# Edge groups of the destination attention: loaded in the graph convolution, coded and split in the first expert layer, transposed in the first attention

## The chip, the cores and the metric

The kernel is one program on one core of a Trainium2 chip. The metric is the time of one execution on the device in microseconds (us), of which the median over several runs is taken; lower is better. A core has five engines that run side by side, each through its own list of instructions in order: PE (TensorE, matrix products), DVE (VectorE), ACT (ScalarE), POOL (GpSimd) and SP (SyncE, which here only issues DMAs). DMAs are issued by SP and ACT on a queue of each, and by POOL where rows are gathered or scattered by index. A `Tile` layer places the instructions: the order in which the Python code traces them is a wish, and an instruction can be placed ahead of others once its data and its space in memory are there.

## What is computed

A network of four layers on a graph of 3125 nodes with 256 features and 100000 edges (`src`, `dst`, sorted by `dst`). Each layer has a graph part and an expert part:

```python
edge_index = jnp.stack([src, dst])
x = x + L0_gnn(layernorm(x), edge_index, edge_weight, ...)     # graph convolution + 2-layer MLP
x = x + L0_ffn(layernorm(x))                                   # 8 experts, 2 per token, 256 wide
x = x + L1_gnn(layernorm(x), edge_index, edge_attr_2, ...)     # attention over sources, 4 heads
x = x + L1_ffn(layernorm(x))                                   # 8 experts, 2 per token, 1024 wide
x = x + L2_gnn(layernorm(x), ..., edge_attr_3, edge_index)     # attention over destinations, 8 heads
x = x + L2_ffn(layernorm(x))                                   # 8 experts, 2 per token
x = x + L3_gnn(layernorm(x), ...)                              # 3 hops
x = x + L3_ffn(layernorm(x))                                   # 8 experts, 1 per token, with a capacity
```

The change concerns what the third graph part (`L2_gnn`) needs of the edges. For each edge it needs the source, the destination, the three attributes of `edge_attr_3`, and, since it takes a maximum over all edges of one destination, the knowledge of which neighbouring edges have the same destination.

## The kernel before

`x` stays in SBUF as 25 tiles of 128 nodes. Constants: `P` = 128, `CH` = 4, `G` = `CH`*`P` = 512 edges in a group, `NU` = 220 groups of edges sorted by destination (a group has edges of one destination tile only), `NCK` = `NU`*`CH` = 880.

The order of the work, with the times at which the profiled execution has it:

1. **Ranks and scatter** (0 to 1340 us). The edges' ranks by source and destination tile are counted, then POOL scatters the 100000 edges with 800 indirect DMAs (L955 in `scatter`) into the DRAM table `chunks`.
2. **Beside the scatter.** `groups_of_dst` works out where each group begins (`es_d`), how many edges it has left (`gd_left`) and the number of the group plus one (`gd_iu1`). `first_layer` makes the first products, `table_of_edges` writes the table of edges `sorted_d`. `load_groups` then loads the 220 groups with 220 DMAs of SP (16 KB each, 128 bytes a partition) into `raw_d` (178 to 379 us). `degrees` sums edge weights by source. Then come the two pieces of the change: `codes_of_groups` makes the gather index `idx_d` (L580), a mask of the real edges (L584), the code (L589 to L591: destination plus group number for real edges, minus the group number for the rest), its store to DRAM (`codes`, L599), and the destination within its tile `lo_d` (L601 to L607). `edge_rows` makes `er_lo` (L617) and splits the three attributes into three BF16 parts each (`split`, L260 to L265), and stores both to DRAM as `er_all` (L626, L627).
3. **Block building** (`blocks`, 518 to 1405 us): the edges are read back from `chunks` in pieces (`ch`) as the scatter gets on, turned into one-hot matrices (`bk_oh`, L1132; `bk_ow`, L1153) and products (L1162, L1165, summed at L1171), and stored as dense 128x128 blocks, `mats`.
4. **Graph convolution** (`gcn`, 1412 to 1745 us): for each of 25 destination tiles a load of 1.6 MB of blocks (`m`, three buffers, on SP), 25 matmuls (L1288), addition and scaling on DVE, a transpose (L1298) and its copy (`h7T`, L1299). In this loop `rows_of_edges` transposes 3 of 69 pieces of `er_all` a tile (PE transpose, copy on DVE and ACT in turn, store on the queue of ACT), after one load of all of `er_all` on the queue of ACT. After tile 2 `penalties` reads `codes` back (`pn_co`), compares neighbours (`pn_pen`, L639, L642) and stores the penalties in 16 DMAs. Then the two dense products follow, hidden layer `hT` of pool `l0g`, product L1317.
5. **First expert part** (`routed`, `moe`, 1735 to 1958 us): the router and the slots of tokens (`slots`, DVE), the store of normalised rows `xrows` (L1650, SP), then 28 groups of tokens in `experts`: weights on SP (L1545 to L1551, three buffers), gathers of rows on POOL (`xb`, L316, three buffers), transposes (L1565), products (L1575, L1582), scatter of results on POOL (L1589). `between(u)` is called after group u and adds the normalised rows to x (L1663).
6. **First attention** (`attention`, 1965 to 3400 us): a front (load of `ch`, L1710, and its transposes, projection weights, results of the experts read back, L1679, layer norm and projection), then `messages`: 276 steps with a load (`lb`, L1776, SP), a one-hot compare (`ot`, L1778, DVE), a gather by matmul (PE), a product (`m`, L1793, DVE), an addition (L1797, POOL), a copy (`ex`, L1798, ACT) and a store (`stash`, L1799, SP). Then come the sums.
7. The second expert part, the third graph part (3515 to 4625 us; it reads `idx_d`, `lo_d`, `lo_rows`, `att_rows`, `pens`), its experts, the hops and the last experts.

The `Tile` pools are stacks: a pool opened where another has been closed uses the same space, and its first writer waits for the last readers there.

Of the kernel before, what the change touches and what calls it, by code (L numbers as in the profile page):

```python
# [10 lines left out]
F32 = mybir.dt.float32  # L11
BF16 = mybir.dt.bfloat16
# [76 lines left out]
class Net:  # L89
# [231 lines left out]
    def sort_edges(self):  # L321
# [3 lines left out]
        with tc.tile_pool(name="sg", bufs=1) as keep:  # L325
# [17 lines left out]
            with tc.tile_pool(name="sr", bufs=1) as early:  # L343
                with tc.tile_pool(name="st", bufs=1) as gpool, \
                        tc.tile_pool(name="st_ps", bufs=1, space=PSUM) as psum, \
                        tc.tile_pool(name="l0x", bufs=2) as xp, tc.tile_pool(name="l0xps", bufs=2, space=PSUM) as xpsum:
                    starts = self.groups_of_dst(early, gpool, psum, wrong)
                    self.first_layer(xp, xpsum)
                    self.table_of_edges(0)
                    self.load_groups(early, starts)  # L350
                with tc.tile_pool(name="dg", bufs=1) as pool, \
                        tc.tile_pool(name="dg_ps", bufs=1, space=PSUM) as psum:
                    self.expert_buffers(pool)
                    self.degrees(pool, psum)
                    self.codes_of_groups(pool)
                    self.edge_rows(pool)
# [142 lines left out]
    def groups_of_dst(self, early, pool, psum, wrong):  # L499
# [54 lines left out]
        left = early.tile([P, NU], F32, name="gd_left")  # L554
        nc.vector.tensor_tensor(left, end, es, op=OP.subtract)
        iu1 = early.tile([P, NU], F32, name="gd_iu1")
        nc.vector.tensor_scalar(iu1, iu, 1.0, None, op0=OP.add)
        self.left, self.iu1 = left, iu1
        return es_i

    def load_groups(self, early, es_i):
# [3 lines left out]
        raw = early.tile([P, NCK, 8], F32, name="raw_d")  # L565
        rawg = raw.rearrange("p (u c) w -> p u c w", c=CH)
        last = []
        for u in range(NU):
            r = self.load_reg(SP, u, last[u - 8] if u >= 8 else None, es_i, 2 * E + G)
            last.append(nc.sync.dma_start(  # L570
                out=rawg[:, u], in_=self.tables[ds(r, G), :].rearrange("(p c) w -> p c w", c=CH)))
        self.raw_g = raw

    def codes_of_groups(self, pool):


        nc, const, raw, end, iu1 = self.nc, self.const, self.raw_g, self.left, self.iu1
# [2131 lines left out]
```

## Time and profile before

| | |
|---|---|
| median of 10 runs | 6101.39 us (6095.77 to 6106.09) |
| the profiled execution | 6100.68 us |
| its span | 6098.8 us |
| busy: PE, DVE, POOL, ACT | 4931.5, 3682.7, 2435.0, 2394.7 us |
| scatters L955 | 800, 984.1 us busy |
| groups' loads, 178 to 379 us | 220 on SP |
| graph convolution | 1412 to 1745 us |
| first experts on PE | 1818 to 1958 us |
| messages of the first attention | 2031 to 2370 us |

The profile comes from one execution. Its span is the time from the first to the last instruction on the engines; the execution's own time is 1.9 us longer. The profile says when each instruction ran and, where an engine was idle, which event ended the idle time (its releaser). "L955" is line 955 of the kernel; "chunks<-tb_pay,tb_row" are the names of what is written and read; "SPq" is the issuing of DMAs by SP. A group line gives a count, the busy time in us with the mean of one in ns, and then the idle time just before, with its releaser. A wait line gives us in total, how many times, and the longest. The granted clock is the share of full speed that PE was given.

### The profile page before, as it was taken

The page shows a single profiled execution, that of the slowest core. Times are in us where ns is not written, and L with a number is a line of the kernel's source. Part 1 is how long each engine was busy: PE and PEld are TensorE (multiplying, and loading weights), DVE is VectorE, ACT ScalarE, POOL GpSimd, SP SyncE. Part 2 cuts the span into 40 slices and gives each one's busy share as a digit, 9 for nine tenths or more (in the row PEclk, how much of TensorE's full clock was granted, in tenths as well). Part 3 has the DMA queues.
Part 4 walks back from the last instruction along what each step waited for, and adds up shares of the span by engine and source line. Part 5 has one row for each costly group of instructions (what it writes and reads, how often), then busy time and mean ns, then how long its engine had stood idle before and what let it go on. Part 6 is the DMA issues. An engine that isn't in the chain of part 4 may idle for free. (4 is left out here: it accounts for less than half of the span.)

```text
span 6098.8 us, 89424 instructions
## 1 busy us (share of the span) xinstructions
PE 4931.5 (81%) x24912; PEld 3978.8 (65%) x24912; DVE 3682.7 (60%) x7420; ACT 2394.7 (39%) x6080; POOL 2435.0 (40%) x2332
## 2 busy tenths in 40 slices
PE   5446777568977787999699789898985999699986
PEld 4334776566855786777588545555554887488775
DVE  6788998672142898999511458888887000432343
ACT  3454777561022212444322366666662222210121
POOL 3778777760006464000022177777770222000021
PEclk8657777668989898999699879999996999799988
DMA  3473234456527574222355476667663653798653
GB/s 83 106 17 35 61 95 112 116 141 174 155 82 214 168 219 153 76 75 75 110 184 180 153 230 196 198 197 202 198 195 98 203 181 128 209 241 238 172 191 121
DMA packets 987725, 912.52 MB, mean 150 GB/s; under 512 B 188483, under 2 KB 897573, under 8 KB 986422
## 3 DMA queue, kind: packets, MB, share of 16 engines
q1 hardware_dynamic: 873858, 716.08, 41.0%
q0 software_dynamic: 84736, 166.99, 11.2%
q10 hardware_dynamic: 28580, 23.10, 1.2%
q8 instruction: 223, 3.65, 0.3%
q14 instruction: 328, 2.69, 0.2%
HBM read 707.87 MB, written 288.94 MB: 163 GB/s over the span
## 5 line engine op out<-in xcount | busy, mean ns | idle before, releaser
L955 POOL DMA_INDIRECT chunks<-tb_pay,tb_row x800 | 984.1, 1230 | 337.1 <-issue 241.4
L316 POOL DMA_INDIRECT xb<-xrows,sl_tok x172 | 168.3, 978 | 1387.7 <-DVE sl_to L1522 1221.4
L316 POOL DMA_INDIRECT g<-table,idx_d x652 | 631.3, 968 | 215.7 <-issue 157.2
L1584 DVE TENSOR_TENSOR yb<-ps_o,eb 128x256 f32<-128x256 f32 x200 | 84.5, 423 | 953.0 <-PE ps_o L1582 934.1
L1575 PE MATMUL ps_h<-xe,ew 128*128 128x256 f32 x2528 | 584.4, 389 | 31.6 <-ACT xe L172 17.4
L1582 PE MATMUL ps_o<-ew,hT 128*128 128x256 f32 x2528 | 562.5, 379 | 0.0
L1171 DVE SCALAR_TENSOR_TENSOR bk_acc<-bk_acc,bk_on,bk_m 128x256 f32<-128x256 f32 x1102 | 527.5, 479 | 51.8 <-DVE bk_acc L1171 0.4
L1575 PEld LDWEIGHTS ps_h<-xe,ew 128*128 128x128 f32 x2528 | 481.4, 193 | 116.7 <-ACT xe L172 32.0
L1855 PE MATMUL ps_a<-rhs,oh 128*128 128x261 f32 x2208 | 510.1, 387 | 31.9 <-ACT rhs L1852 24.9
L2485 PE MATMUL ps_a<-h,m 128*128 128x512 f32 x1875 | 485.1, 408 | 56.9 <-DVE ln_st L202 45.7
L1165 PE MATMUL bk_m<-bk_ow,bk_oh 128*128 128x128 f32 x2208 | 512.5, 372 | 13.8 <-ACT bk_ow L1153 13.8
L1582 PEld LDWEIGHTS ps_o<-ew,hT 128*128 128x128 f32 x2528 | 477.1, 190 | 69.1 <-ACT hT L1577 4.2
L1577 ACT ACTIVATE hT<-ps_h,eb 128x256 f32<-128x256 f32 x632 | 297.2, 474 | 572.9 <-PE ps_h L1575 566.5
L1162 PE MATMUL bk_m<-bk_oh 128*128 128x128 f32 x1104 | 305.6, 369 | 242.3 <-DVE bk_acc L1171 222.1
L1855 PEld LDWEIGHTS ps_a<-rhs,oh 128*128 128x128 f32 x2208 | 409.9, 190 | 131.9 <-ACT oh_abs L1840 38.9
L2288 PE MATMUL ps_a<-wt,oh 128*128 128x264 f32 x1664 | 453.1, 419 | 48.2 <-ACT l_iota L2248 25.2
L1153 ACT ACTIVATE bk_ow<-bk_oh,ch 128x128 f32<-128x128 f32 x1104 | 363.9, 389 | 274.3 <-DVE bk_oh L1132 259.9
L2485 PEld LDWEIGHTS ps_a<-h,m 128*128 128x128 f32 x1875 | 350.9, 190 | 134.9 <-ACT h L2430 54.1
L1165 PEld LDWEIGHTS bk_m<-bk_ow,bk_oh 128*128 128x128 f32 x2208 | 425.4, 269 | 14.4 <-ACT bk_ow L1153 14.1
L1162 PEld LDWEIGHTS bk_m<-bk_oh 128*128 128x128 f32 x1104 | 236.6, 265 | 298.4 <-issue 177.1
L2288 PEld LDWEIGHTS ps_a<-wt,oh 128*128 128x128 f32 x1664 | 329.8, 204 | 145.5 <-DVE wt L2278 44.6
L2094 DVE SCALAR_TENSOR_TENSOR tt<-er,col,ps_hd 128x512 f32<-128x512 f32 x416 | 293.2, 743 | 178.2 <-PE ps_hd L2093 163.7
(611 smaller groups left out, 8996.5 us busy)
## 6 DMA issues: line engine op xcount, KB each, us to landing
m<-mats SPq DMA_DIRECT2D x99, 1600.0 KB
mats<-bk_acc SPq DMA_DIRECT2D x1103, 128.0 KB
ew<-in_L_ffn_W_dram SPq DMA_DIRECT2D x116, 1024.0 KB
hd<-rows SPq DMA_DIRECT2D x208, 256.0 KB
stash<-m SPq DMA_DIRECT2D x276, 136.0 KB
ms<-stash SPq DMA_DIRECT2D x276, 136.0 KB
lb<-src_rows SPq DMA_DIRECT2D x276, 128.0 KB
ew<-in_L_ffn_w_dram SPq DMA_DIRECT2D x28, 1024.0 KB
```

Source lines behind the costliest of these rows:

```text
L316: return self.nc.gpsimd.indirect_dma_start(out=out, out_offset=None, in_=table, in_offset=bass.IndirectOffsetOnAxis(ap=idx, axis=0))
L955: sc = nc.gpsimd.indirect_dma_start(out=self.chunks, out_offset=bass.IndirectOffsetOnAxis(ap=self.row[:, k : k + 1], axis=0), in_=self.pay ...
L1153: nc.scalar.mul(ow[:, i], of[:, k % 4 + i, 0, :], ch[:, c + i, 2:3])
L1162: nc.tensor.matmul(ps[:, i, 0, :], oh[:, c0 + i, 0, :], oh[:, c0 + i, 1, :], start=True, stop=True)
L1165: nc.tensor.matmul(ps[:, i, 1, :], of[:, c0 + i, 1, :], ow[:, i], start=True, stop=True)
L1171: nc.vector.scalar_tensor_tensor(new, acc[0], goes_on[:, k + i : k + i + 1], ps[:, i], op0=OP.mult, op1=OP.add)
L1575: nc.tensor.matmul(ps, w1[:, k, f * P : (f + 1) * P], xe[:, k, :], start=k == 0, stop=k == 1)
L1577: nc.scalar.activation(hT[:, f, :], ps, act, bias=b1[:, f : f + 1])
L1582: nc.tensor.matmul(ps, hT[:, f, j * P : (j + 1) * P], w2[:, f, :], start=f == 0, stop=f == FP - 1)
L1855: nc.tensor.matmul(ps, oh[:, c, :], rhs[:, c, :], start=c == 0, stop=c == CH - 1)
L2288: nc.tensor.matmul(po, oh[:, c, :], wt[:, c, :], start=c == 0, stop=c == CH - 1)
L2485: nc.tensor.matmul(pa.rearrange("p i d -> p (i d)"), m[:, j, :], h[:, j].rearrange("p i d -> p (i d)"), start=j == 0, stop=j == NT - 1)
```

## The change

- `groups_of_dst` writes `gd_left` and `gd_iu1` as one tile to DRAM (`left_d`) and keeps the starts of the groups.
- `load_groups` becomes a generator with one load at a time. It is moved into the loop of `gcn`, nine loads a tile, into a pool `sr` (28 KB a partition) that is opened at the start of `gcn` and kept until the first experts are done.
- `codes_of_groups` is called after group 1 of the first experts, `edge_rows` after group 3, both in a pool `cg` (some 41 KB a partition). `left_d` is read back for it.
- `rows_of_edges` is moved from `gcn` to the messages of the first attention, one piece every third step; it loads each piece of `er_all` by itself on SP, copies on ACT and stores on SP.
- `penalties` is moved from `gcn` to just before the messages. The message buffers in PSUM (`l1gps`) go from 4 to 3, and two small ones for the transposes are added.

```diff
@@ -340,20 +340,16 @@
                     self.rows_of_table(pool, self.tables[E + G :], rows)
                 self.ranks(keep, rows)
             self.load_x()
-            with tc.tile_pool(name="sr", bufs=1) as early:
-                with tc.tile_pool(name="st", bufs=1) as gpool, \
-                        tc.tile_pool(name="st_ps", bufs=1, space=PSUM) as psum, \
-                        tc.tile_pool(name="l0x", bufs=2) as xp, tc.tile_pool(name="l0xps", bufs=2, space=PSUM) as xpsum:
-                    starts = self.groups_of_dst(early, gpool, psum, wrong)
-                    self.first_layer(xp, xpsum)
-                    self.table_of_edges(0)
-                    self.load_groups(early, starts)
-                with tc.tile_pool(name="dg", bufs=1) as pool, \
-                        tc.tile_pool(name="dg_ps", bufs=1, space=PSUM) as psum:
-                    self.expert_buffers(pool)
-                    self.degrees(pool, psum)
-                    self.codes_of_groups(pool)
-                    self.edge_rows(pool)
+            with tc.tile_pool(name="st", bufs=1) as gpool, \
+                    tc.tile_pool(name="st_ps", bufs=1, space=PSUM) as psum, \
+                    tc.tile_pool(name="l0x", bufs=2) as xp, tc.tile_pool(name="l0xps", bufs=2, space=PSUM) as xpsum:
+                self.groups_of_dst(gpool, psum, wrong)
+                self.first_layer(xp, xpsum)
+                self.table_of_edges(0)
+            with tc.tile_pool(name="dg", bufs=1) as pool, \
+                    tc.tile_pool(name="dg_ps", bufs=1, space=PSUM) as psum:
+                self.expert_buffers(pool)
+                self.degrees(pool, psum)
             self.gcn_inputs()
             self.blocks()
 
@@ -496,7 +492,7 @@
                     tc.add_to_no_dep_group(f"radix{i}", sc.ins)
         nc.sync.dma_start(out=table[:E], in_=tabs[3])
 
-    def groups_of_dst(self, early, pool, psum, wrong):
+    def groups_of_dst(self, pool, psum, wrong):
 
 
         nc, const = self.nc, self.const
@@ -551,30 +547,33 @@
         nc.vector.tensor_scalar(other, wrong[0:1], 0.0, float(E + G), op0=OP.is_gt, op1=OP.mult)
         es_i = const.tile([1, NU], I32, name="es_d")
         nc.vector.tensor_scalar(es_i, es[0:1], other, None, op0=OP.add)
-        left = early.tile([P, NU], F32, name="gd_left")
-        nc.vector.tensor_tensor(left, end, es, op=OP.subtract)
-        iu1 = early.tile([P, NU], F32, name="gd_iu1")
-        nc.vector.tensor_scalar(iu1, iu, 1.0, None, op0=OP.add)
-        self.left, self.iu1 = left, iu1
-        return es_i
-
-    def load_groups(self, early, es_i):
+        left = pool.tile([P, 2, NU], F32, name="gd_left")
+        nc.vector.tensor_tensor(left[:, 0], end, es, op=OP.subtract)
+        nc.vector.tensor_scalar(left[:, 1], iu, 1.0, None, op0=OP.add)
+        self.left = self.dram.tile([P, 2, NU], F32, name="left_d")
+        nc.sync.dma_start(out=self.left, in_=left)
+        self.starts = es_i
+
+    def load_groups(self, pool):
 
         nc = self.nc
         SP = mybir.EngineType.SP
-        raw = early.tile([P, NCK, 8], F32, name="raw_d")
-        rawg = raw.rearrange("p (u c) w -> p u c w", c=CH)
+        self.raw_g = pool.tile([P, NCK, 8], F32, name="raw_d")
+        rawg = self.raw_g.rearrange("p (u c) w -> p u c w", c=CH)
         last = []
         for u in range(NU):
-            r = self.load_reg(SP, u, last[u - 8] if u >= 8 else None, es_i, 2 * E + G)
+            r = self.load_reg(SP, u, last[u - 8] if u >= 8 else None, self.starts, 2 * E + G)
             last.append(nc.sync.dma_start(
                 out=rawg[:, u], in_=self.tables[ds(r, G), :].rearrange("(p c) w -> p c w", c=CH)))
-        self.raw_g = raw
+            yield
 
     def codes_of_groups(self, pool):
 
 
-        nc, const, raw, end, iu1 = self.nc, self.const, self.raw_g, self.left, self.iu1
+        nc, const, raw = self.nc, self.const, self.raw_g
+        left = pool.tile([P, 2, NU], F32, name="gd_left")
+        nc.sync.dma_start(out=left, in_=self.left)
+        end, iu1 = left[:, 0], left[:, 1]
         rawg = raw.rearrange("p (u c) w -> p u c w", c=CH)
         self.idx_d = const.tile([P, NCK], I32, name="idx_d")
         nc.vector.tensor_copy(self.idx_d, raw[:, :, 4])
@@ -653,17 +652,17 @@
     def rows_of_edges(self, pool, psum):
 
         nc = self.nc
-        er = pool.tile([P, NCK * 10], BF16, name="er")
-        nc.scalar.dma_start(out=er, in_=self.er_all)
         i = 0
-        for src, dst, n in ((er[:, :NCK], self.lo_rows, NCK), (er[:, NCK:], self.att_rows, NCK * 9)):
+        for src, dst, n in ((self.er_all[:, :NCK], self.lo_rows, NCK), (self.er_all[:, NCK:], self.att_rows, NCK * 9)):
             for c0 in range(0, n, P):
                 m = min(P, n - c0)
-                pt = psum.tile([P, P], BF16, name="ps_h")
-                nc.tensor.transpose(pt[:m], src[:, c0 : c0 + m], self.identb)
+                er = pool.tile([P, P], BF16, name="er", bufs=4)
+                nc.sync.dma_start(out=er[:, :m], in_=src[:, c0 : c0 + m])
+                pt = psum.tile([P, P], BF16, name="ps_h", bufs=2)
+                nc.tensor.transpose(pt[:m], er[:, :m], self.identb)
                 row = pool.tile([P, P], BF16, name="er_row", bufs=4)
-                self.copy(i, row[:m], pt[:m])
-                nc.scalar.dma_start(out=dst[c0 : c0 + m], in_=row[:m])
+                nc.scalar.copy(row[:m], pt[:m])
+                nc.sync.dma_start(out=dst[c0 : c0 + m], in_=row[:m])
                 i += 1
                 yield
 
@@ -1268,6 +1267,8 @@
     def gcn(self):
         nc, tc, a = self.nc, self.tc, self.a
         w1, bc, y = self.first_inputs
+        self.edges = ExitStack()
+        groups = self.load_groups(self.edges.enter_context(tc.tile_pool(name="sr", bufs=1)))
         with ExitStack() as st:
             gp = st.enter_context(tc.tile_pool(name="l0g", bufs=1))
             gT = gp.tile([P, 2, NT * P], F32, name="hT")
@@ -1275,7 +1276,6 @@
             nc.scalar.dma_start(out=w2, in_=a["L0_gnn_W2"].rearrange("(k p) f -> p k f", p=P))
             with tc.tile_pool(name="l0h", bufs=1) as hp, \
                     tc.tile_pool(name="l0hps", bufs=2, space=PSUM) as psum:
-                rows = self.rows_of_edges(hp, psum)
                 hT = hp.tile([P, 2, NT * P], F32, name="h7T")
                 for t in range(NT):
                     m = hp.tile([P, NT, P], F32, name="m", bufs=3)
@@ -1286,10 +1286,8 @@
                     pa = psum.tile([P, D], F32, name="ps_a")
                     for i in range(NT):
                         nc.tensor.matmul(pa, m[:, i, :], y[:, i, :], start=i == 0, stop=i == NT - 1)
-                    for _ in range(3):
-                        next(rows, None)
-                    if t == 2:
-                        self.penalties(hp)
+                    for _ in range(NU // NT + 1):
+                        next(groups, None)
                     acc = hp.tile([P, D], F32, name="acc", bufs=2)
                     nc.vector.tensor_tensor(acc, pa, y[:, t, :], op=OP.add)
                     nc.vector.tensor_scalar(acc, acc, self.dinv[:, t : t + 1], None, op0=OP.mult)
@@ -1657,12 +1655,19 @@
         st, xn, m1, m2, tok, to, eid = self.chosen
         xrows, ybuf = self.xrows[layer], self.ybuf[layer]
         if layer == 0:
+            cp = self.edges.enter_context(tc.tile_pool(name="cg", bufs=1))
+
             def between(u):
+                if u == 1:
+                    self.codes_of_groups(cp)
+                if u == 3:
+                    self.edge_rows(cp)
                 if u < 5:
                     part = self.x[:, 5 * u : 5 * u + 5, :]
                     nc.vector.tensor_tensor(part, part, xn[:, 5 * u : 5 * u + 5, :], op=OP.add)
 
             self.experts(eid, tok, to, xrows, ybuf, "L0_ffn_w", "L0_ffn_b", 256, AF.Gelu, USUAL_NG, between=between)
+            self.edges.close()
         elif layer == 1:
             self.experts(eid, tok, to, xrows, ybuf, "L1_ffn_W", "L1_ffn_b", 1024, AF.Gelu, USUAL_NG,
                          (a["L1_ffn_ln_g"], a["L1_ffn_ln_b"]))
@@ -1763,8 +1768,11 @@
                 nc.vector.tensor_tensor(e, e, no[:, : k1 - k0, None].to_broadcast([P, k1 - k0, H]), op=OP.add)
                 nc.vector.tensor_reduce(top[:, i, :], e.rearrange("p c h -> p h c"), AX.X, OP.max)
 
-            with tc.tile_pool(name="l1g", bufs=6) as gp, tc.tile_pool(name="l1m", bufs=4) as mp, \
-                    tc.tile_pool(name="l1gps", bufs=4, space=PSUM) as psum:
+            with tc.tile_pool(name="pn", bufs=1) as pp, \
+                    tc.tile_pool(name="l1g", bufs=6) as gp, tc.tile_pool(name="l1m", bufs=4) as mp, \
+                    tc.tile_pool(name="l1gps", bufs=3, space=PSUM) as psum:
+                erows = self.rows_of_edges(pp, psum)
+
                 def messages(q0, q1, parts):
                     done = {}
                     for i, (k0, k1) in parts.items():
@@ -1778,6 +1786,8 @@
                             nc.vector.tensor_scalar(oh, lb, self.pidx, None, op0=OP.is_equal)
                             ohs[q] = oh
                             regs[q] = self.load_regs(PE, src_tile, q * CH, CH, last.get(q - 3))
+                        if q % 3 == 2:
+                            next(erows, None)
                         if q0 <= q - 1 < q1:
                             oh = ohs.pop(q - 1)
                             ps = psum.tile([P, CH, 256], F32, name="ps_g")
@@ -1800,8 +1810,11 @@
                             if q - 2 in done:
                                 settle(*done[q - 2])
 
+                self.penalties(pp)
                 part = USUAL_NKB // QS
                 messages(0, USUAL_NKB // CH, {i: (i * part, (i + 1) * part) for i in range(QS)})
+                for _ in erows:
+                    pass
                 n = nc.values_load(self.n_chunks_i[0:1, 0:1], min_val=0, max_val=NKB)
                 with tc.If(n > USUAL_NKB):
                     messages(USUAL_NKB // CH, NKB // CH, {QS: (USUAL_NKB, NKB)})
```

## Prediction

> **What bounds the kernel now.** I read the profiled execution stage by stage, first its page, then busy time by stretches, then the waits and the order of single instructions in the stages that the change touches. That execution took 6100.68 us, 1.9 us more than its span of 6098.8; the runs shown have a median of 6101.39, so a change worked out from the trace is added to 6100.7. About 0.2% (12 us) is what a measurement of this kernel can tell from no change.
>
> Until about 1340 us POOL scatters the edges into `chunks`, 800 times. These are the groups of POOL between 180 and 380 us, while the 220 group loads run on SP, and after them between 386 and 484 us (count, then busy us and mean ns, then idle and what ended it):
>
> ```profile
> L955 POOL DMA_INDIRECT chunks<-tb_pay,tb_row x133 | 159.8, 1201 | 40.6 <-issue 40.6
> ```
> ```profile
> L955 POOL DMA_INDIRECT chunks<-tb_pay,tb_row x43 | 75.0, 1744 | 23.5 <-issue 12.2 <-DMA chunks<-tb_pay,tb_row 11.3
> ```
>
> A scatter costs 200/133 = 1.50 us in the first stretch and 98/43 = 2.28 in the second. The block building behind it waits for this stream; DVE's waits between 1000 and 1412 us (us, times, longest):
>
> ```profile
> DVE bk_oh L1132 <- DMA ch<-chunks: 83.2, 11, 13.1
> ```
>
> The loads of `ch` are issued 1.3 to 1.5 us after the scatter that they need, up to the last but one. So an earlier start of the building gives nothing, and a shorter scatter stream gives all of it.
>
> The slow stretch holds the pieces that the change moves. SP's issues there (start, us):
>
> ```profile
> 413.70 0.38 SPq L599 DMA_DIRECT2D codes<-gd_code  x1
> 435.59 39.56 SPq L626 DMA_DIRECT2D er_all<-er_lo  x1
> 475.25 0.38 SPq L627 DMA_DIRECT2D er_all<-er_parts  x1
> ```
>
> The store of the codes writes 16 bytes at a time, 28160 packets. The next store of SP could not be issued until 475.15: SP is held for 61.5 us, 61.5 x 16 / 28160 = 35 ns a packet.
>
> The later stages are read from busy time by stretch (length, then PE, PEld, DVE, ACT, POOL with counts, granted clock, DMA share, GB/s):
>
> ```profile
> 1450.00:1700.00 250.00, 250.00 (x1220) 214.69 (x1219) 35.01 (x121) 8.78 (x33) 0.00 (x0) 1.00 0.55 148
> ...
> 1818.00:1958.00 140.00, 121.38 (x560) 94.27 (x560) 34.95 (x83) 38.17 (x85) 102.71 (x104) 0.97 0.74 220
> ...
> 2031.00:2370.00 339.00, 297.42 (x2140) 270.95 (x2141) 317.23 (x551) 54.48 (x267) 227.60 (x268) 0.96 0.68 213
> ```
>
> The graph convolution is bound by PE, the messages of the first attention by DVE (317 of 339 us), and the experts by PE and POOL together.
>
> **1. The scatter stretch: -21 us.** The change takes 16 DVE operations out of 390 to 465 us, with the rows idx_d 0.94, is_lt 1.75, code 1.75 + 1.74 + 1.06, destinations 0.95 + 0.88 + 0.60 + 1.74 + 0.61, er_lo 0.87, and the split of the attributes 2.63 + 4.90 + 1.50 + 2.90 + 1.52: 26.3 us of DVE. It takes their stores too. 43 scatters at 1.50 are 64.7 us, so the stretch lost 33.3. Two long scatters stay, since they lie beside the additions and products of x and y, which stay: 7.62 us at 465.21 and 6.65 at 474.63, with 0.30 of idle each against 1.50, 6.4 + 5.5 = 11.9. What goes is 33.3 - 11.9 = 21.4: 11.3 of it two waits for scatters' own DMAs while the codes drained, the rest scatters of 2.6 to 4.5 us beside single DVE operations. Bounds: -30 (the two neighbours shorten as well) and -5 (whatever runs there next slows POOL as much). The group loads themselves gave POOL nothing back: 1.50 us is the pace beside them.
>
> The Trainium skill, "SBUF — State Buffer", section "SBUF: two separate sides", states that a DVE operation with two SBUF inputs and a GpSimd operation that reads SBUF exclude each other for a whole instruction. That fits the 2.6 to 4.5 us rows, but by it alone casts with one input would cost POOL less, and the gain would be nearer -17; the sum keeps the measured -21.
>
> **2. The graph convolution: -13 us.** PE's waits between 1412 and 1460 us, and DVE's:
>
> ```profile
> PE ps_tr L1298 <- DVE h7T L1299: 7.6, 1, 7.6
> ```
> ```profile
> DVE pn_pen L642 <- DMA pn_co<-codes: 7.9, 1, 7.9
> ```
>
> The penalties, called after tile 2, hold DVE for the codes, and PE waits for the DVE copy behind them. That goes with its after-effect: 42 matmuls then took 11.95 us instead of 9.23. With 69 transposes of 0.055 us (3.8) it makes 7.6 + 2.7 + 3.8 = 14.1. I take 13, since L1294's and L1299's waits for PE remain. New on SP are 9 group loads a tile. 220 took 200.6 us, 0.91 each, and their 128-byte packets cost 12.9% of 16 engines in those 200 us, 13 ns each. Nine are 8.2 us of SP, beside 0.4 for a load of m; a tile takes PE 11.29. It fits if they stand evenly between the loads of m. Bounds: -14, and +90 if many stand ahead of one (rival D).
>
> **3. Codes in the experts: +28 us.** The codes are traced after group 1, the split after group 3. But instructions run in front of their place in the text: the addition of L1663, traced between groups 0 to 4, starts at 1747.92, and a load of the attention stands among the weights. SP's issues around it:
>
> ```profile
> 1801.59 0.34 SPq L1551 DMA_DIRECT2D eb<-in_L_ffn_b_dram  x1
> 1808.81 0.33 SPq L1710 DMA_DIRECT2D ch<-chunks  x1
> 1825.64 0.38 SPq L1545 DMA_DIRECT2D ew<-in_L_ffn_w_dram  x1
> ```
>
> So I expect the codes when their space is free, that is when the last product of the convolution has read its hidden layer (about 1768), after some 7 us of DVE operations between the router's: the store is issued near 1780. It holds SP for the 61.5 us of before, to about 1841. The weights of groups 0 to 2 are issued at 1794.87 to 1801.9 now; behind the store they come 40 to 46 us late and land by about 1850. PE starts its experts at 1818 now, the first weight matmul at 1822: +28. Nothing gives it back: POOL already runs its three buffers ahead and then waits for PE (gathers to 1816.8, the next at 1822.0), and from 1828 it is busy without a break. If the store stands between the weights of group 2 and of group 3 (1825.64), groups 0 to 2 run, at 5 us each, and group 3 waits: up to +50. DVE's 26.3 us lie in the shadow of this wait; without it they cost about 10, since DVE is busy for 31 of the 50 us before 1818. Bounds: 0 and +55.
>
> The skill, "DMA: Bandwidth & Descriptors", "Queues, rings and completion order", says that SP has one ring on each DMA engine and that descriptors are consumed there in order, which speaks against the change: the weights cannot pass the store. By its "Specifications" anything under 512 B misses line rate alike; the rows differ, 13 ns a packet for loads of 128 B against 35 for stores of 16.
>
> **4. Front of the attention: +8 us.** Its load of `ch` (issued at 1808.81 now) and its weights now lie where the groups, the codes and their pools are held until the experts end (PE's at 1958). Chains that now end early, the rows of sources and the weights of the projection, start about 1960 instead of beside the experts. The first y is used at 1969.9 now, and the front's own work lasts to 2031. Bounds: 0 (all beside y) and +20. I take 8, nearer the lower, as y<-ybuf keeps SP until 1990 anyway.
>
> **5. Messages: +15 us.** There are 69 loads and 69 stores more on SP, 69 copies more on ACT (54 us busy of 339), 69 transposes on PE. SP's instructions run 0.35 to 0.46 each, 138 x 0.45 = 62 us. SP waits in this stage for about 107 of 339 us, mostly for POOL's m (68.4), so the time is there; but each store waits for its copy with the loads of `lb` and the stores of the messages queued behind it. DVE waits 12.8 us for `lb` now. The 16 stores of penalties (0.72 each, 11.5) stand in the same queue, and their DVE work (3.3 us) on the bounding engine. With one message buffer less in PSUM (3 for 4) lags are worse covered. Bounds: +3 (the DVE work) and +50 (most of the 62). I take a quarter of the issue time, 15.
>
> **6. Elsewhere: +2 us**, the new store of `left` and its reload.
>
> Sum: -21 - 13 + 28 + 8 + 15 + 2 = +19, 6100.7 + 19 = **6120**.
>
> **Rivals.** A, faster, about 6078: the new DMAs drain where SP has nothing urgent. Its place is the end of the convolution: the codes' pool lies over buffers that are free after the last tile (about 1700), so the store is issued by 1733 and has drained by 1795, ahead of the weights. Step 3 is then 0, and with the messages' DMAs in SP's 107 us of waits (+3) and the front between 0 and 8 the sum is -21 - 13 + 0 + 3 + 2 + (0 to 8) = -29 to -21: 6072 to 6080. For it: early work does run early, and PE alone is busy from 1450 to 1700. Against it: the hidden layer is read until 1768. It decides from 1733 on.
> B, the same, about 6097: the store comes near 1750 and costs half (+14), the messages +5: -21 - 13 + 14 + 8 + 5 + 2 = -5 (6096); or the store is early as in A, but front and messages cost the +23 of the forecast: -9 (6092).
> C, the forecast: 6114 to 6150.
> D, much slower, 6165 to 6200: more than 12 group loads stand between two loads of m (12 x 0.91 = 11 us, a tile), PE starves about 9 us a tile for 8 to 10 tiles, +80 in place of part of -13. Or SP becomes the bound of the messages (+50). For it: nothing binds the 220 loads to their tiles; against it: m has three buffers.
> E, that the change does not do what it says (the codes run as late as written, after group 3): the store then meets later weights, with the same price of 40 to 55; it is part of C.
>
> **How the numbers follow.** A 0.24, B 0.22, C with E 0.40, D 0.14. Faster 0.24, same 0.22, slower 0.54. The range from 6074 to 6185 leaves out about 2 in 10: the lower end of A and the far part of D. C's own range is 6114 to 6150.
>
> **What would show it.** Step 1: scatters at 1.5 us between 390 and 464 and the last one ending near 1318 instead of 1338. Step 2: no wait of 7.6 us, 25 tiles at 11.3. Step 3: an SP issue of some 40 us or a weight load more than 20 us late at the first experts, PE's wait there for weights. Step 4: first lb behind 2035. Step 5: DVE waits for lb above 12.8 us and a stage longer than 339. The forecast is wrong if the store of the codes drains where SP has nothing urgent, or if m is late.

## The result and the profile after

The changed kernel takes 6351.88 us (median of 8 runs, 6345.14 to 6356.97) where the kernel before takes 6103.63 (28 runs): a ratio of 1.0406, 95% interval 1.0397 to 1.0415. Slower was forecast; +248 us instead of +19 was not, and the range (to 6185) does not hold it.

The profiled spans are 6098.8 and 6345.0 us, 246.2 apart. Six marks that both traces have, and the end, split that difference:

| mark | before, us | after, us | difference | added in this stage |
|---|---|---|---|---|
| last product of the block building starts on DVE (L1171, now L1170) | 1403.1 | 1377.2 | -25.9 | -25.9 |
| first matmul of the convolution (L1288) | 1417.3 | 1576.5 | +159.2 | **+185.1** |
| its last | 1711.8 | 1853.0 | +141.2 | -18.0 |
| first gather of the experts | 1809.6 | 1951.6 | +142.0 | +0.8 |
| first load of their results (y) | 1965.5 | 2169.8 | +204.3 | **+62.3** |
| first sum of the attention | 2401.6 | 2646.3 | +244.7 | **+40.4** |
| end of the span | 6098.8 | 6345.0 | +246.2 | +1.5 |

**The scatter stretch** did what the first step said. The groups of POOL from 386 to 484 us, after:

```profile
L954 POOL DMA_INDIRECT chunks<-tb_pay,tb_row x63 | 80.9, 1284 | 19.2 <-issue 19.2
```

63 scatters fit where 43 did, at 98/63 = 1.56 us, and no wait for a scatter's own DMA is left. DVE still waits for `ch`, 77.9 us in 11 times between 1000 and 1412, so POOL still bounds. From the first to the last start of the 800 scatters it is 1240.9 us before and 1215.0 after. The pages show where the 25.9 us come from, 14.8 from the scatters' own busy time and 11.2 from POOL's idle time before them (before, then after):

```profile
L955 POOL DMA_INDIRECT chunks<-tb_pay,tb_row x800 | 984.1, 1230 | 337.1 <-issue 241.4
```
```profile
L954 POOL DMA_INDIRECT chunks<-tb_pay,tb_row x800 | 969.3, 1212 | 325.9 <-issue 242.9
```

**Then PE stands still.** Before, SP went from the stores of blocks to the loads of blocks within 8 us. Its issues from 1400 to 1640 us, merged (start, duration of the whole run of them, line, count), and PE's longest wait from 1375 to 1800:

```profile
1404.78 0.07 SPq L1176 DMA_DIRECT2D mats<-bk_carry  x1
1412.30 14.43 SPq L1285 DMA_DIRECT2D m<-mats  x5
...
1456.51 177.32 SPq L1285 DMA_DIRECT2D m<-mats  x17
```
```profile
PE ps_a L1288 <- DMA m<-mats: 17.8, 1, 17.8
```

The same after, SP's issues from 1340 to 1800 us:

```profile
1340.42 38.53 SPq L1175 DMA_DIRECT2D mats<-bk_acc  x63
1379.18 0.07 SPq L1175 DMA_DIRECT2D mats<-bk_carry  x1
1382.27 184.32 SPq L566 DMA_DIRECT2D raw_d<-sorted_d  x220
1571.48 227.26 SPq L1285 DMA_DIRECT2D m<-mats  x25
```
```profile
PE ps_a L1288 <- DMA m<-mats: 203.8, 1, 203.8
```

All 220 group loads stand between the last store of blocks and the first load of blocks. None is left for the loop in which they are written. The convolution itself, once it starts, is 18.0 us shorter.

**The first experts** have the store of the codes between their weights, behind those of groups 0 to 3. SP's issues (start, us), and PE's longest wait from 1940 to 2170 us:

```profile
1975.92 0.38 SPq L598 DMA_DIRECT2D codes<-gd_code  x1
1976.55 53.57 SPq L1543 DMA_DIRECT2D ew<-in_L_ffn_w_dram  x1
2030.22 0.41 SPq L625 DMA_DIRECT2D er_all<-er_lo  x1
```
```profile
PE ps_h L1573 <- DMA ew<-in_L_ffn_w_dram: 46.9, 1, 46.9
```

PE's only entry for weights before, from 1800 to 1966 us:

```profile
PE ps_tr L1565 <- DMA ew<-in_L_ffn_w_dram: 5.3, 5, 1.1
```

The weight load behind the store, that of group 4, takes 53.6 us to issue, as `er_lo` took 39.6 before. The 62.3 us of this stage are not all of the codes. From the first to the last product of the experts it is 54 us longer (190.3 for 136.2). Another 8 stand between the last scatter of results and the first load of y (12.5 us for 4.3). There the loads of the attention's weights stand now, 11 to 14 us ahead of that first load of y, once the experts are done; before, SP issued them 117 to 123 us ahead of it. Whether they are what holds y was not tested.

**The messages** wait for their sources. DVE's waits from the first load of sources to the first sum, before and then after:

```profile
DVE ot L1778 <- DMA lb<-src_rows: 13.3, 22, 2.0
```
```profile
DVE ot L1786 <- DMA lb<-src_rows: 49.0, 96, 1.4
```

22 waits of 13.3 us have become 96 of 49.0.

### The profile page after: what moved, and what is told of

Read it like the earlier page. It is cut to its first block, busy times and chain, and to the rows that moved or that the text cites. A ratio compares the mean times of both kernels' runs of the same rounds, so it can differ in the third digit from the quotient of the medians.

```text
span 6345.0 us, 89274 instructions
## 1 busy us (share of the span) xinstructions
PE 4948.4 (78%) x24912; PEld 3988.8 (63%) x24912; DVE 3679.9 (58%) x7386; ACT 2394.4 (38%) x6114; POOL 2425.0 (38%) x2332
## 5 line engine op out<-in xcount | busy, mean ns | idle before, releaser
L954 POOL DMA_INDIRECT chunks<-tb_pay,tb_row x800 | 969.3, 1212 | 325.9 <-issue 242.9
L1573 PE MATMUL ps_h<-xe,ew 128*128 128x256 f32 x2528 | 589.6, 391 | 76.8 <-DMA ew<-in_L_ffn_w_dram 46.9
L1170 DVE SCALAR_TENSOR_TENSOR bk_acc<-bk_acc,bk_on,bk_m 128x256 f32<-128x256 f32 x1102 | 527.5, 479 | 52.2 <-PE bk_m L1164 0.4
L1288 PE MATMUL ps_a<-y,m 128*128 128x256 f32 x1250 | 277.0, 381 | 203.8 <-DMA m<-mats 203.8
L1164 PEld LDWEIGHTS bk_m<-bk_ow,bk_oh 128*128 128x128 f32 x2208 | 423.1, 268 | 13.3 <-ACT bk_ow L1152 13.1
```

Of the source, the lines that this page charges most:

```text
L954: sc = nc.gpsimd.indirect_dma_start(out=self.chunks, out_offset=bass.IndirectOffsetOnAxis(ap=self.row[:, k : k + 1], axis=0), in_=self.pay ...
L1164: nc.tensor.matmul(ps[:, i, 1, :], of[:, c0 + i, 1, :], ow[:, i], start=True, stop=True)
L1170: nc.vector.scalar_tensor_tensor(new, acc[0], goes_on[:, k + i : k + i + 1], ps[:, i], op0=OP.mult, op1=OP.add)
L1573: nc.tensor.matmul(ps, w1[:, k, f * P : (f + 1) * P], xe[:, k, :], start=k == 0, stop=k == 1)
```

## The experiments

The experiments ran on chips on which the kernel before takes 6696 us (the first four kernels) and 6910 to 6918 us (the others). The changed kernel itself ran on none of them. PE's granted clock is lower there. From 600 to 1000 us it was 0.74 on the chip of the result; on the others, in kernels that leave this stretch as it was (three message buffers; penalties alone), it was 0.52 and 0.50, and in the third graph part 0.79 to 0.81 where it was 0.96. The clock need not be the whole difference: from its first to its last summing product (L2288) the third graph part is 435 to 448 us longer in these two runs, and PE is busy for only 166 of them; what fills the rest was not looked into.

POOL does not bound the block building there: from 600 to 1600 us DVE's longest waits in it are for PE's `bk_m`, and none is for `ch`. So the size of what the change gains before the convolution does not carry over, nor do the times in us that some expectations name; they are for the chip of the result.

Each ratio below is to the kernel before on the same chip, and the stages are compared by their lengths: the pause from the last product of the building to the first matmul of the convolution, the convolution from its first to its last matmul of blocks, the experts from the first gather to the first load of y, and the attention from there to the first sum. Each length is from one profiled execution. The experts are some 30 to 38 us longer on those chips, the other three as before; the runs with three message buffers and with codes turned in the kernel before stand for "before" there.

| kernel | pause | convolution | experts | attention | ratio to before |
|---|---|---|---|---|---|
| before | 14.2 | 294.5 | 155.9 | 436.1 | 1 |
| changed | 199.3 | 276.5 | 218.2 | 476.5 | 1.0406 |
| *chip of 6696* | | | | | |
| before, three message buffers | 14.4 | 293.4 | 186.7 | 438.1 | 1.0001 (0.9986 to 1.0016) |
| changed, loads behind each tile's blocks | 12.3 | 327.6 | 240.3 | 480.2 | 1.0137 (1.0104 to 1.0170) |
| changed, codes on ACT's queue | 198.4 | 276.6 | 244.1 | 475.6 | 1.0365 (1.0331 to 1.0399) |
| changed, rows on ACT's queue | 199.1 | 277.0 | 241.2 | 461.9 | 1.0347 (1.0313 to 1.0380) |
| *chips of 6910 to 6918* | | | | | |
| before, codes turned | 14.0 | 294.2 | 191.7 | 440.6 | 0.9982 (0.9968 to 0.9996) |
| changed, codes turned | 199.0 | 276.5 | 202.0 | 488.9 | 1.0254 (1.0228 to 1.0281) |
| changed, rows in fours | 199.3 | 277.8 | 247.7 | 460.5 | 1.0294 (1.0277 to 1.0311) |
| changed, loads on ACT's queue | 196.9 | 276.9 | 250.2 | 482.8 | 1.0299 (1.0276 to 1.0322) |
| changed, these three | 196.0 | 277.4 | 202.9 | 463.3 | 1.0210 (1.0193 to 1.0227) |
| these three, loads behind the first blocks | 12.6 | 279.9 | 200.1 | 460.9 | **0.9946** (0.9926 to 0.9966) |
| the same, rows behind the first sources | 12.6 | 285.8 | 190.1 | 473.1 | 0.9954 (0.9935 to 0.9972) |
| before, rows and penalties in messages | 14.1 | 277.3 | 185.6 | 485.6 | 1.0031 (1.0016 to 1.0046) |
| before, rows alone in messages | 14.0 | 279.0 | 193.9 | 475.6 | 1.0062 (1.0045 to 1.0079) |
| before, penalties alone ahead of messages | 13.1 | 283.7 | 191.3 | 436.8 | 0.9988 (0.9975 to 1.0001) |
| before, rows in fours alone in messages | 13.8 | 278.5 | 187.9 | 448.6 | 1.0008 (0.9998 to 1.0019) |

My theory at the start: SP's queue, in order, is the cause at all three places. The rivals were the DMA engines themselves, and other resources (a PSUM buffer, DVE beside POOL).

### The group loads

**Behind each tile's blocks**, in the changed kernel (`behind` binds only the place in the order):

```diff
+            self.behind(last[-1], self.m_load, "after the tile's blocks")
             yield
...
-                        (nc.scalar if i == 5 or i == 15 else nc.sync).dma_start(out=m[:, i:i1], in_=of[:, i:i1])
+                        ld = (nc.scalar if i == 5 or i == 15 else nc.sync).dma_start(out=m[:, i:i1], in_=of[:, i:i1])
+                    self.m_load = ld
```

> The changed kernel, with the nine group loads of each tile made to follow that tile's load of blocks on SP. Theory (SP's order): the first load of blocks no longer stands behind 220 group loads, PE starts the convolution some 185 to 190 us earlier, 6155 to 6175 us, and PE's 203.8 us wait falls below 25. Rival (nine loads at 0.91 us beside the loads of blocks are too much for SP or the DMA engines, and tiles take longer than 11.3 us): 6200 to 6300.

The pause fell from 199 to 12.3 us, so the order is what made it. The convolution was 327.6 us, 51 longer than in the changed kernel, but not for want of blocks: PE waits for `m` only at the start (16.6 us in all). It is busy 27 us longer, mostly since the next products (L1306) now run between the tiles, and it waits 16.3 us for `acc` and 7.6 for `h7T` in a new order. From the last block matmul to the first gather it is 81.1 us for 98.6, so 17 of the 51 come back. The theory held for the pause; the tiles got longer as the rival said, but not for its reason.

**On ACT's queue**, unbound:

```diff
-            r = self.load_reg(SP, u, last[u - 8] if u >= 8 else None, self.starts, 2 * E + G)
-            last.append(nc.sync.dma_start(
+            r = self.load_reg(ACT, u, last[u - 8] if u >= 8 else None, self.starts, 2 * E + G)
+            last.append(nc.scalar.dma_start(
```

> The changed kernel, with the 220 group loads on the queue of ACT instead of SP, free of any order to the loads of blocks. Theory (it is the order on SP's queue): the convolution starts within 10 us of the end of the building and lasts 275 to 295 us from its first to its last matmul of blocks, ratio to before 1.008 to 1.013. Rival (220 loads and the loads of blocks compete on the DMA engines, or share completion semaphores): the convolution is 20 us or more longer than that, ratio above 1.014.

The pause is as good as unchanged at 196.9 us: it outlasts the move off SP's queue, and my theory that this queue alone makes it fell. ACT's issues, SP's, and SP's waits:

```profile
1598.57 188.39 ACTq L565 DMA_DIRECT2D raw_d<-sorted_d  x220
```
```profile
1601.49 0.07 SPq L1174 DMA_DIRECT2D mats<-bk_carry  x1
1791.89 29.80 SPq L1284 DMA_DIRECT2D m<-mats  x7
```
```profile
SPq L1217 <- SPq L1217: 183.8, 8, 175.9
```

SP issues nothing for 190 us, and what it waits at is the conditional tail of `blocks` (L1217 there, L1218 in the changed kernel), the blocks for chunks beyond the usual number. They aren't needed for this data, but the branch is there. In the trace SP reaches that branch at 1604.42, when ACT has begun its 220 loads, and at the branch's end SP waits in turn on all eight semaphores that the completions of the DMAs of SP and ACT count; the loads of blocks come behind it. So they wait for every group load that was placed ahead of the branch. In the changed kernel SP issues those 220 loads itself and is held by that already (184.3 us); its wait at the branch is then 2.4 us. Either of the two is enough.

**Behind the first blocks only**, on ACT's queue, with the two other cures told below:

```diff
+            self.behind(last[-1], self.m_load, "after the first blocks")
             yield
...
+                    if t == 0:
+                        self.m_load = ld
```

> The changed kernel, with the codes turned, the rows in fours and the group loads on ACT's queue, all three. Theory (three separate queues of DMAs make the whole loss, and what stays is the gain before the convolution): -185, -45 and -30 us from 6352 are about 6092, ratio to before 0.995 to 1.002. Rival (the moved work costs its time wherever it stands): above 1.005.

> The kernel with codes turned, rows in fours and group loads on ACT's queue, with the group loads made to follow the first load of blocks, which puts them behind the conditional tail of the block building. Theory (the loads of blocks waited for the join at the end of that conditional, which waits for every DMA in flight, and not for SP's queue or the DMA engines): the wait of 199 us is gone, the convolution lasts 275 to 300 us from first to last matmul of blocks, ratio to before 0.992 to 0.997. Rival (220 loads compete with the loads of blocks while the convolution runs): the convolution is over 310 us, ratio above 0.998.

Without the binding the three cures give 1.0210, since the pause stays (196.0 us); with it 0.9946: 7061 us (6918 before) and 6876 (6913 before), 185 apart, or 181 against the kernel before on each chip, about the size of the pause. This last version is 0.5% faster than the kernel before on its chip; on the chip of the result it was not run. PE's wait at the start of the convolution, bound:

```profile
PE ps_a L1301 <- DMA m<-mats: 17.0, 1, 17.0
```

and the convolution is 279.9 us with ACT's queue busy with the 220 group loads from 1593.8 for 213.4 us: beside the blocks they cost PE nearly nothing (276.5 to 277.8 in the changed kernels that have issued them all before it). The rival of contention is out.

### The codes

**On ACT's queue**, in the changed kernel (the store L598 with `nc.scalar` for `nc.sync`):

> The changed kernel, with the store of the codes on the queue of ACT instead of SP. Theory (the weights stand behind the store in SP's order): PE's wait of 46.9 us for weights goes, 6300 to 6312 us. Rival (the 28160 packets hold the DMA engines themselves, whoever issues them): the wait stays above 30 us, 6335 to 6355.

PE's wait is still 39.5 us, and the experts 244.1 (240.3 and 241.2 with the store on SP): SP's order alone is not it. But it is not simply the busy DMA engines of the rival either. PE's and SP's longest waits from 2010 to 2260 us:

```profile
PE ps_h L1573 <- DMA ew<-in_L_ffn_w_dram: 39.5, 1, 39.5
```
```profile
SPq L1549 <- DMA codes<-gd_code: 51.7, 1, 51.7
```

SP waits for the landing of the codes. The program has eight completion semaphores for the DMAs of SP and ACT together and takes them in turn, so a DMA waits until the one that had its semaphore before has landed. Here the store is issued at 2040.6 and has landed at 2101.0; the DMA of SP that is next to have its semaphore is issued at 2101.2. A slow DMA stops both queues a few DMAs later.

**Turned on PE**, so that the store is 220 rows of 2 KB:

```diff
+        for u0 in range(0, NU, P):
+            n = min(P, NU - u0)
+            ct = pool.tile([P, P, CH], F32, name="gd_ct", bufs=2)
+            for c in range(0, CH, 2):
+                pt = self.eps.tile([P, 2, P], F32, name="ps_tr")
+                for k in range(2):
+                    nc.tensor.transpose(pt[:n, k], code[:, u0 : u0 + n, c + k], self.ident)
+                nc.scalar.copy(ct[:n, :, c : c + 2].rearrange("u p k -> u k p"), pt[:n])
+            nc.sync.dma_start(out=self.codes[1 + u0 * G : 1 + (u0 + n) * G].rearrange("(u w) -> u w", w=G),
+                              in_=ct[:n].rearrange("u p c -> u (p c)"))
```

> The changed kernel, with the codes turned on PE (8 transposes) before they are stored, so that the store has 220 rows of 2 KB instead of 28160 pieces of 16 bytes. Theory (the small packets of the store hold the DMA engines, and every DMA that follows on any queue comes late): PE's wait for weights of 39 to 47 us in the first experts falls below 10, the experts' stage is 40 to 50 us shorter than in the changed kernel, ratio to before 1.032 to 1.034 where the changed kernel has 1.0406. Rival (DVE's 26 us and the gathers that it slows make the experts late): the stage loses less than 15 us, ratio above 1.037.

No wait for weights is left among PE's longest. The experts are 202.0 us, where two other changed kernels on these chips have 247.7 and 250.2: 46 to 48 us less. The small pieces were it. Some 10 us over "before" stay (191.7); as I read it, because the first gathers stand beside DVE's casts and splits, which no run took away. POOL's first two in that run:

```profile
2173.96 3.36 POOL L316 DMA_INDIRECT xb<-xrows,sl_tok  x1 [858.18 <-DVE gd_ends L594]
2177.62 5.15 POOL L316 DMA_INDIRECT xb<-xrows,sl_tok  x1 [0.30 <-issue]
```

against 0.95 us for a gather alone. The ratio, 1.0254, cannot be set beside 1.0406 from another chip, so the expectation's ratios stay untested; the length of its stage and its wait are as the theory had them.

**Turned in the kernel before**, where it stands in the scatter stretch:

> The kernel before, with the codes turned on PE before their store (220 rows of 2 KB) and nothing else. Theory (the drain of the small packets costs POOL 11 us of waits in the scatter stretch, and DVE beside POOL the rest): 8 to 14 us faster, ratio 0.9975 to 0.999, the two long waits of POOL gone. Rival (all of the loss is DVE beside POOL): within 4 us, and the scatter stretch as long as before.

0.9982 (0.9968 to 0.9996), inside what was expected. On this chip POOL does not bound the building, so I read the scatter stream itself. From the first to the last start of its 800 scatters it takes 1233.5 us here, and 1239.5 to 1245.0 in the four kernels on these chips that leave the stretch as it was: 6 to 11.5 us less. POOL's waits for its scatters' own DMAs from 300 to 620 us, 12.3 to 14.4 us in those four, are gone. The page shows the idle time of the changed kernel and the busy time of before:

```profile
L965 POOL DMA_INDIRECT chunks<-tb_pay,tb_row x800 | 989.0, 1236 | 325.4 <-issue 242.8
```

So the store accounts for the idle time, 11.2 of the 25.9 us on the chip of the result. The other 14.8, scatters that are shorter without DVE's operations beside them, are the larger part; no run took away these operations alone.

### The messages

**Three buffers for four**, in the kernel before (`bufs=3` in `l1gps`):

> The kernel before, with three message buffers in PSUM instead of four and nothing else. Theory (SP bounds the messages of the changed kernel): within 5 us of before, 6096 to 6108. Rival (the lost buffer does it): 25 to 37 us slower, 6128 to 6140.

1.0001, attention 438.1 us: the lost buffer costs nothing.

**Rows on ACT's queue**, in the changed kernel (load and store of `rows_of_edges` with `nc.scalar`):

> The changed kernel, with the 69 loads and 69 stores of rows_of_edges on the queue of ACT instead of SP. Theory (SP's issue time bounds the messages): the messages lose 25 to 37 us, 6315 to 6327 us. Rival (three message buffers in PSUM for four, or the transposes on PE, slow them): 6345 to 6355, the stage as long as in the changed kernel.

The stage is 461.9 us for 475.6 to 480.2 in the other two changed kernels on this chip, 14 to 18 less and 24 above before: about half. DVE's waits for `lb` go to 36.2.

**Rows in fours**, in the changed kernel:

```diff
-                er = pool.tile([P, P], BF16, name="er", bufs=4)
-                nc.sync.dma_start(out=er[:, :m], in_=src[:, c0 : c0 + m])
+        er = pool.tile([P, NCK * 10], BF16, name="er")
+        nc.sync.dma_start(out=er, in_=self.er_all)
...
+                for i in range(k):
+                    nc.tensor.transpose(pt[:m, i], src[:, c0 + i * P : c0 + i * P + m], self.identb)
+                nc.scalar.copy(row[:m, :k], pt[:m, :k])
+                nc.sync.dma_start(out=dst[c0 : c0 + k * m].rearrange("(k p) f -> p k f", p=m), in_=row[:m, :k])
```

> The changed kernel, with the edge rows loaded at once and transposed four to a PSUM tile, one copy and one store for four: 1 load and 18 stores for 69 and 69, all on SP. Theory (the number of DMAs on SP bounds the messages): the stage of the messages is 28 to 40 us shorter than in the changed kernel, ratio to before 1.034 to 1.036. Rival (the transposes on PE and copies on ACT, or the penalties in front, make it longer): less than 15 us, above 1.038.

460.5 us for 482.8 and 488.9: 22 to 28 less, and 20 above before. **Their load behind the first sources, penalties later**:

> As the run with the group loads behind the first blocks, and in the messages the load of the edge rows behind the loads of sources 0 to 7, the penalties after message 60. Theory (what the fours left in the front, 20 to 25 us over before, is the load of 2.2 MB and the penalties ahead of the first messages): 10 to 25 us faster than that run, ratio 0.989 to 0.995. Rival (the front is long because pools are held until the experts end): within 5 us of that run.

No gain: 0.9954 for 0.9946, attention 473.1 for 460.9. Nothing speaks for the theory that this load and the penalties fill the front.

**One part alone, in the kernel before**: rows and penalties together, the rows alone, the penalties alone, the rows alone in fours:

> The kernel before with one part of the change: rows_of_edges and the penalties in the messages as in the changed kernel, the rest as before. Theory (the messages pay 38 to 42 us, the convolution gains 13 to 17): 21 to 29 us slower, ratio 1.003 to 1.005. Rival (the messages are longer in the changed kernel for another reason, such as the pools held by the first experts): less than 8 us slower, ratio below 1.0015.

> The kernel before with only rows_of_edges in the messages as in the changed kernel; the penalties stay in the convolution. Theory (the 138 DMAs of the rows on SP make the sources late): from the first load of y to the first sum 465 to 480 us, where before has 436 to 441 and both parts together 486, DVE's waits for lb above 40 us. Rival (the penalties make most of it): below 455 us.

> The kernel before with only the penalties ahead of the messages; the rows stay in the convolution. Theory (rows): the same stretch 438 to 455 us, the convolution without its wait of 7.6 us. Rival (penalties): above 460 us.

> The kernel before with only the rows in the messages, loaded at once and taken four at a time (1 load and 18 stores on SP). Theory (the number of DMAs): the stretch 438 to 452 us. Rival (whatever the number, the load of 2.2 MB, the transposes and copies cost as much): above 460 us.

Against 440.6 the attention has +45.0, +35.0, -3.8 and +8.0 us. Against 294.2 the convolution has -16.9, -15.2, -10.5 and -15.7. DVE's waits for sources in the first of these, from the first load of y:

```profile
DVE ot L1776 <- DMA lb<-src_rows: 54.5, 101, 1.4
```

and with the penalties alone:

```profile
DVE ot L1777 <- DMA lb<-src_rows: 18.3, 28, 1.6
```

The rows with their 138 DMAs are the cost, 35 us; taken four at a time 8 are left. (The fours also take 18 copies for 69, which no run separates from the DMAs; that DVE waits for `lb` speaks for the DMAs.) The penalties alone cost nothing in this stage, and with the rows 10 more. Penalties alone give 0.9988 (0.9975 to 1.0001), not distinct from no change. For the rows alone the whole kernel, 1.0062, loses more than these stages add up to (20 us are 0.3%); where the rest goes is open. What makes the 20 us that stay in the changed kernel with rows in fours, where the same part alone leaves 8, is open too: the penalties with them, or the pools that the experts hold until their end, which put off the weights of the attention.

## Why the prediction was wrong

- **The bound of the first 1400 us and step 1**: right. -21 forecast, -25.9 measured, and it is the scatter stream: 1240.9 us before, 1215.0 after. Of the split, the waits held (11.3 worked out, 11.2 measured), and the scatters beside DVE gave more than the 10 (14.8). The remark that casts with one input would cost POOL less, and the -17 with it, did not hold: the kernel before already has a scatter of 3.13 us beside such a cast (L260, at 440.07), against 1.18 of its neighbours.
- **Step 2, the convolution's own length**: right. 14.1 was worked out, 18.0 measured; the penalties alone give 10.5 for 7.6 + 2.7, rows and penalties 16.9.
- **Step 2, "It fits if they stand evenly between the loads of m"**: this is the step that failed, with 185 of the 248 us. The loads were not in the loop at all. Step 3 used the rule that instructions run in front of their place in the text as soon as data and space are there; step 2 did not apply it to the 220 loads, the first of which starts 3 us after the last store of blocks. Rival D named the mechanism (group loads ahead of a load of m) but priced it at 9 us a tile for 8 to 10 tiles; all 220 ahead of the first are 220 x 0.91 = 200 us by the row that the prediction itself used, and 184.3 were measured. And neither saw that a second thing keeps the loads of blocks behind them, besides SP's own order: the end of a conditional between them, as the run on ACT's queue shows.
- **Step 3, the codes**: the mechanism (weights late by the drain of the codes) was right, the size was not: 54 us longer from the first to the last product of the experts for 28, at the edge of the bound of 55, and 62.3 in the whole stage. The drain stood later than assumed, between the weights of groups 3 and 4, which is rival E's place and at its price; so PE waited 46.9 us instead of 28. The other 7 fit the first gathers beside DVE's casts, four of them 2.1 to 5.2 us long instead of 0.95, which the text laid in the shadow of the wait; this is argued, not shown. "The weights cannot pass the store" fits what SP's queue did, where the next DMA took 53.6 us to issue, but is not the whole reason: with the store on another queue they are as late.
- **Steps 4 and 5, front and messages**: 23 forecast, 40.4 measured, and 8 more ahead of the first load of y, inside the two bounds (3 to 70). Step 4 was right that the attention's weights would start only when the experts end. In step 5 the quarter of the 62 us of issue time was mis-sized: the rows alone cost 35, more than half. SP's 107 us of waits were not free time: DVE's waits for `lb` rose from 13.3 to 49.0 us.
- **The range**: its top came from D's 80 us for part of the loads, though the trace had the price of all 220, 200 us.

## What to carry to other kernels

Ask of each moved load what is the earliest point at which its data and space allow it, and what stands between that point and the place where it is written: in this program the end of a conditional waits for all DMAs of SP and ACT, so that every load that gets ahead of it holds up all that follow (184 us here). Look at a transfer's pieces and at how long it is in flight, and not only at its bytes or its queue: here 440 KB in pieces of 16 bytes delayed what came after them, at the old place and at the new, there on either queue; in rows of 2 KB, after eight transposes, PE's wait for weights and POOL's waits for its own DMAs were gone. Work put into the gaps of an engine that feeds the bound was not free here (35 us for 69 loads and 69 stores): count its DMAs, and gather them before moving them (8 us for 1 load and 18 stores).

## What the runs showed of the hardware that I had not expected

- A wait of a queue need not come from that queue: with the 220 loads on ACT's queue SP stood still for 176 us, with the codes on ACT's queue for 51.7 us, both times for semaphores that DMAs of both queues share in this program.
- A store of 440 KB in 16-byte pieces held SP's next DMA for 53.6 us in the issue; on ACT's queue it took 60.4 us from its issue to its landing.
- 220 loads of 16 KB in 128-byte pieces beside 1.6 MB a tile of blocks slowed the convolution by 2 to 3.4 us in all (279.9 for 276.5 to 277.8).
- Which engine bounds a stage can differ from chip to chip: in the block building DVE waits 83.2 us for `ch` behind POOL's scatters on the chip with a granted clock of 0.74, and on one with 0.52 not for them at all but 137 us for PE's products.
